# Windowed attention: the products of weights and values for two heads in one matmul, split into two halves of a step

## The chip, the cores and the metric

The kernel runs on one core of a Trainium2 chip. Its engines work side by side, each through its own queue in program order: TensorE (PE in the profile, its weight loads PEld), VectorE (DVE), ScalarE (ACT), GpSimd (POOL) and SyncE (SP), which here only issues DMAs. The metric is the device time of one execution in microseconds (us); lower is better. Matmul results land in PSUM and are copied from there to SBUF by ACT or DVE.

## The reference

The whole is a network of four blocks on 16 sequences of 512 tokens with 128 features. Each block is `x + layernorm(block(layernorm(x)))`. Only the first, an attention with a sliding window, is touched:

```python
H, D, window_size = (16, 64, 32)
B, T, C = x.shape                      # 16, 512, 128
xn = rms_norm(x)
q, k, v = jnp.split(xn @ w_qkv.T, 3, axis=-1)
...
q = apply_rope(q, cos, sin)
k = apply_rope(k, cos, sin)
attn = jnp.einsum('bhqd,bhkd->bhqk', q, k) * scale
mask = (q_pos >= k_pos) & (q_pos - k_pos <= window_size)
attn = softmax(jnp.where(mask, attn, NEG))
out = jnp.einsum('bhqk,bhkd->bhqd', attn, v)
return out.transpose(0, 2, 1, 3).reshape(B, T, H * D) @ w_out.T
```

A query sees itself and the 32 tokens before it. The line that the change is about is the product of `attn` and `v`. After this block come a mixture of eight experts, a second attention and a feed-forward block.

## The kernel before, in words

**Tiling.** `windowed_attention` (from line 296 on) works in units: a unit u is one sequence (u // 2) and one half of its 16 heads, so there are NU = 32. A unit has NP = 4 pairs of heads, p = 0 to 3, and each pair is a step n = 4u + p; there are 128. Queries stand in eight blocks of QT = 64, named by j (0 to 3, of 128 tokens) and c (0 or 1, which half). A block of 64 queries needs KW = 96 keys: its own 64 and the 32 before. All data are float32.

**Values.** `values(u, j)` (L416 on) multiplies tokens by the value weights into pv; ACT copies it to `v_odd` (L423). The 96 keys of a c = 1 block are rows of one `v_odd` tile. Those of a c = 0 block are not, so when j = 3 is done three DMAs on SP's queue (L426, L427, L428) put together `v_even`, a shifted copy. Their calls stand in step p = 0 of the unit that they serve (`values(u, 3)`), the products that read them begin in step p = 3.

**One step n** of the schedule, which is written out by hand at the end of the function, calls in this order:

1. `weigh(n - 1)`: DVE sums the exponentials (L467), takes reciprocals (L469); POOL multiplies (L470).
2. `score(n)`: PE adds the mask and the products of q and k into s (L438, L447); DVE takes the negated row maxima nmax (L452); ACT takes eight exponentials of 128x96 into pr (L458). s has one buffer, so the s of the next step waits for these exponentials.
3. `project(...)`: PE projects a quarter of q or k of a unit further on into pq (L398), DVE multiplies it by cosines and sines (L402, L404), POOL adds (L407), SP writes the result to DRAM (`far`, L408); one step later SP reads it back in another layout into qT or kT (L411). The tile t that far is read from has three buffers.
4. `values(u, 3)` if p = 0, `values(u + 1, 1)` if p = 3, `project_out` (pf, L512) if p is odd.
5. `turn(n - 2)`: PE transposes pr (pt, L481), ACT copies the result to prT (L483). PSUM tiles of pv, pf, pt and some transposes share three buffers.
6. `products(n - 3)`: PE multiplies the weights prT by the values into po (L498), DVE copies po to oT (L502). po has one buffer.
7. `values(u + 1, 0)` if p = 2, `values(u + 1, 2)` if p = 3, and small tasks of layer norms that come due.

So the products of pair n come three steps after its scores. In `products` the two heads r of the pair are separate matmuls: head r has 64 columns of the values as stationary side, its 64 queries as moving side, and writes partitions 64r to 64r + 63 of po. That makes 4 x 2 x 2 = 16 matmuls a step. A float32 matmul shows as two records in the trace, so the profile counts 32 a step.

`project_out(u, part)` later reads oT, all four pairs of a unit, as stationary side. It is not changed.

Of the kernel before, what the change touches and what calls it, by code (L numbers as in the profile page):

```python
# [20 lines left out]
F32 = mybir.dt.float32  # L21
# [10 lines left out]
P = 128  # L32
B, T, C = 16, 512, 128
NTB = T // P
# [5 lines left out]
H0, D0, WIN = 16, 64, 32  # L40
QT = 64
KW = QT + WIN
# [183 lines left out]
def run_due(tasks, now):  # L226

    for task in list(tasks):
        if task[0] <= now:
            lag = next(task[1], None)  # L230
            if lag is None:
                tasks.remove(task)
            else:
                task[0] = now + lag
# [61 lines left out]
def windowed_attention(net):  # L296
# [12 lines left out]
    nc, tc, a = net.nc, net.tc, net.a  # L309
    NU, NP, NC = 2 * B, H0 // 4, H0 * D0 // P  # L310
    HALF = D0 // 2
    with ExitStack() as ctx:
# [9 lines left out]
        with tc.tile_pool(name="wload", bufs=1) as lp, tc.tile_pool(name="ps_w", bufs=2, space=PSUM) as ps:  # L322
# [13 lines left out]
            for g in range(NG):  # L336
# [4 lines left out]
                s = D0 ** -0.5 if g < 2 else 1.0  # L341
# [17 lines left out]
        v_odd = [wp.tile([P, NTB, T], F32, name=f"v_odd{i}") for i in range(2)]  # L359
        v_even = [wp.tile([P, NTB, T], F32, name=f"v_even{i}") for i in range(2)]  # L360
# [14 lines left out]
        ps_o = ctx.enter_context(tc.tile_pool(name="ps0_o", bufs=1, space=PSUM))  # L375
        xnT, ao, oT, pairs, tasks = {}, {}, {}, {}, []
# [4 lines left out]
        def prepare(b):  # L381

            z = tok.tile([P, NTB, C], F32, name=f"z_a{b}", tag="z")
            yield from normed_in(net, net.x[b], f"a{b}", z, by_scalar, 1.0 + RMS_EPS, LN_EPS * RMS_EPS)
            yield 2
            pz = transposed(net, ps_x, z, f"a{b}", "x")
            x = tok.tile([P, T + WIN], F32, name=f"xnT_{b}", tag="xnT")
            nc.scalar.copy(x[:, :T], pz)
            nc.scalar.copy(x[:, T:], pz[:, :WIN])
            xnT[b] = x  # L390
# [39 lines left out]
        def score(n):  # L430

            u, p = divmod(n, NP)
            q, k = qT[u % 2], kT[u % 2]
            s = ps_s.tile([P, 2, T], F32, name=f"s_{n}", tag="s")
            for c in range(2):
                for r in range(2):
                    at = slice(64 * r, 64 * r + 64)
                    nc.tensor.matmul(  # L438
                        s[64 * c : 64 * c + 64, r, : NTB * KW], lhsT=eye[at, at],
                        rhs=mask[at, c].rearrange("p j k -> p (j k)"), start=True, stop=False,  # L440
                    )
            for j in range(NTB):
                for c in range(2):
                    t = j * P + c * 64
                    for r in range(2):
                        at = slice(64 * r, 64 * r + 64)
                        nc.tensor.matmul(  # L447
                            s[64 * c : 64 * c + 64, r, j * KW : (j + 1) * KW], lhsT=q[at, p, t : t + 64],
                            rhs=k[at, p, t : t + KW], start=False, stop=(j == NTB - 1),
                        )  # L450
            nmax = sp.tile([P, 2, NTB], F32, name=f"nmax_{n}", tag="nmax")
            nc.vector.tensor_reduce(  # L452
                nmax, s[:, :, : NTB * KW].rearrange("p r (j k) -> p r j k", k=KW), AX.X, ALU.max, negate=True
            )
            pr = ep.tile([P, 2, NTB, KW], F32, name=f"pr_{n}", tag="pr")
            for r in range(2):
                for j in range(NTB):
                    nc.scalar.activation(  # L458
                        pr[:, r, j, :], s[:, r, j * KW : (j + 1) * KW], AF.Exp, bias=nmax[:, r, j : j + 1]
                    )  # L460
            pairs[n] = pr

        def weigh(n):

            pr = pairs[n].rearrange("p r j k -> p (r j) k")
            sums = sp.tile([P, 2 * NTB], F32, name=f"sums_{n}", tag="sums")
            nc.vector.tensor_reduce(sums, pr, AX.X, ALU.add)  # L467
            rc = sp.tile([P, 2 * NTB], F32, name=f"rc_{n}", tag="rc")
            nc.vector.reciprocal(rc, sums)  # L469
            nc.gpsimd.tensor_tensor(pr, pr, per_token(rc, KW), ALU.mult)  # L470
# [12 lines left out]
                nc.scalar.copy(prT[:KW, c], pt[c][:KW])  # L483
            pairs[n] = prT

        def products(n):
            u, p = divmod(n, NP)
            prT = pairs.pop(n)
            if p == 0:
                oT[u] = up.tile([P, NP, T], F32, name=f"oT_{u}", tag="oT")  # L490
            po = ps_o.tile([P, T], F32, name=f"po_{n}", tag="o")
            for j in range(NTB):
                for c in range(2):
                    v = (v_even, v_odd)[c][u % 2]
                    t = j * P + c * 64
                    for r in range(2):
                        at = (2 * p + r) * D0
                        nc.tensor.matmul(  # L498
                            po[D0 * r : D0 * r + D0, t : t + 64], lhsT=v[:KW, j, at : at + D0],
                            rhs=prT[:KW, c, r, j, :], start=True, stop=True,  # L500
                        )
            nc.vector.tensor_copy(oT[u][:, p, :], po)  # L502

        def project_out(u, part):

# [48 lines left out]
        with tc.manual_schedule():  # L554
            for _ in prepare(0):
                pass
            for n in range(-NP - 2, NP * (NU + 2) + 16):
                u, p = divmod(n, NP)
                if 0 <= n - 1 < NP * NU:
                    weigh(n - 1)  # L560
                if 0 <= n < NP * NU:
                    score(n)
                ahead, k = divmod(n + NP + 2, NP)
                if ahead < NU:
                    kind, g = ((1, 0), (0, 0), (1, 1), (0, 1))[k]
                    task = project(ahead, kind, g)
                    tasks.append([n + next(task), task])
                if 0 <= u < NU and p == 0:
                    values(u, 3)
                if 0 <= u + 1 < NU and p == 3:  # L570
                    values(u + 1, 1)
                if p % 2 and 0 <= u - 2 + p // 2 < NU:

                    project_out(u - 2 + p // 2, 1 - p // 2)
                    if p == 1 and u % 2:
                        tasks.append([n, close((u - 2) // 2)])
                if 0 <= n - 2 < NP * NU:
                    turn(n - 2)
                if 0 <= n - 3 < NP * NU:
                    products(n - 3)  # L580
                if 0 <= u + 1 < NU and p >= 2:
                    values(u + 1, 2 * (p - 2))
                if p == 0 and u % 2 and (u + 3) // 2 < B:
                    tasks.append([n, prepare((u + 3) // 2)])
                run_due(tasks, n)
            assert not tasks
# [904 lines left out]
```

## Time and profile before

| what | us |
|---|---|
| median of 3 runs | 2530.02 |
| lowest and highest of them | 2494.01, 2530.4 |
| the profiled execution's own time | 2521.29 |
| its span, first to last instruction | 2518.7 |

The mean clock granted to TensorE in the profiled execution was 0.901 of full speed. The first attention takes nearly the first 1020 us. Three windows of it, by the view of windows: the window, its length, then busy us and number of instructions for PE, PEld, DVE, ACT and POOL, then the granted clock, the share of the DMA engines and GB/s:

```profile
300.00:500.00 200.00, 183.17 (x2657) 122.02 (x2653) 158.48 (x278) 110.74 (x343) 131.36 (x114) 0.98 0.57 175
500.00:700.00 200.00, 186.55 (x2715) 124.69 (x2713) 156.02 (x280) 108.70 (x335) 130.75 (x111) 0.97 0.57 169
700.00:900.00 200.00, 185.74 (x2643) 122.50 (x2642) 156.41 (x279) 113.08 (x348) 129.06 (x109) 0.97 0.56 173
```

The stage is even: the three windows are alike. Groups by line from 300 to 700 us, 54 steps (engine, operation, tiles, shapes, count; busy us in all, mean ns of one; idle us before them and what ended it):

```profile
L498 PE MATMUL po<-prT,v_even 96*64 96x64 f32 x870 | 58.0, 232 | 2.5 <-DMA v_even<-v_odd 2.5
L498 PE MATMUL po<-prT,v_odd 96*64 96x64 f32 x872 | 55.6, 226 | 0.0
L502 DVE COPY oT<-po 128x512 f32<-128x512 f32 x54 | 37.0, 685 | 24.1 <-PE po L498 24.0
L520 ACT COPY ao<-pf 128x256 f32<-128x256 f32 x13 | 5.0, 388 | 3.5 <-PE pf L512 3.5
```

A mean of one matmul includes its way through the array, where it overlaps its neighbours; the time that a group of matmuls takes is read from the timeline or the chain of waits.

### The profile page before, as it was taken

Reading aid. Unit: us, or ns where it says so; the run is one execution under the profiler, and the core shown is the slowest. Engines: PE = TensorE matmul, PEld = TensorE weight load, DVE = VectorE, ACT = ScalarE, POOL = GpSimd, SP = SyncE. Lnnn points to the kernel's source line nnn. Section 1 sums busy time; section 2 is a strip of 40 time slices with the busy share of each in tenths; the row PEclk is TensorE's granted clock in tenths of the full one; section 3 lists DMA queues with packets and bytes.
Section 4 is the critical chain, followed back from the end, with each engine's and each line's share of the span. In section 5 each row is a group of like instructions: output and inputs, shape, how many; then the busy total and the mean of one; then the engine's idle time right before and its main releaser. Section 6 shows DMA issues by size and latency. Waiting matters only on the chain.

```text
span 2518.7 us, 54547 instructions
## 1 busy us (share of the span) xinstructions
PE 2086.6 (83%) x21337; PEld 1215.0 (48%) x21337; DVE 1886.4 (75%) x3732; ACT 1383.0 (55%) x3189; POOL 1360.0 (54%) x1338
## 2 busy tenths in 40 slices
PE   5898989999999998236799269999999999998876
PEld 2565656666666566126689123333333333332544
DVE  4777777777888775487861578888888888881886
ACT  1555555555555555113334127777777777775885
POOL 3566666666666664634442334555555565311888
PEclk8999999999999999555579659999999999995999
DMA  6555555555555554101112233333343323321001
GB/s 185 176 173 160 172 170 167 179 168 171 169 178 175 169 172 141 38 13 27 40 51 79 69 67 90 115 92 91 96 117 101 95 83 106 110 61 34 12 26 34
DMA packets 163900, 275.31 MB, mean 109 GB/s; under 512 B 20226, under 2 KB 64572, under 8 KB 158524
## 3 DMA queue, kind: packets, MB, share of 16 engines
q1 hardware_dynamic: 157632, 259.32, 34.6%
q0 software_dynamic: 4096, 8.40, 1.3%
q10 hardware_dynamic: 1916, 4.12, 0.6%
q8 instruction: 168, 2.75, 0.5%
q14 instruction: 88, 0.72, 0.1%
HBM read 133.49 MB, written 114.03 MB: 98 GB/s over the span
## 4 chain that ended last, share of the span: by engine, by line
PE 35%; DVE 24%; DMA 22%; ACT 10%; POOL 5%; issue 2%; SPq 1%; POOLq 0%; DVEq 0%; ACTq 0%
DMA far<-t 17%; PE po L1183 9%; PE sT L1169 6%; DVE nm L1138 5%; ACT ex L1175 4%; DMA v_even<-v_odd 3%; PE s L1135 3%; PE ph L760 2%; PE pq L398 2%; PE po L760 2%; DVE hit L834 2%; DVE t L402 2%; DVE t L404 1%; PE pqk L1067 1%; PE po L498 1%
## 5 line engine op out<-in xcount | busy, mean ns | idle before, releaser
L1138 DVE TENSOR_REDUCE nm<-s 128x2 f32<-128x1024 f32 x512 | 609.9, 1214 | 71.9 <-PE s L1135 66.9
L1175 ACT ACTIVATE ex<-sT 128x512 f32<-128x512 f32 x1024 | 531.1, 604 | 183.6 <-PE sT L1169 183.2
L407 POOL TENSOR_TENSOR t<-t,t 128x512 f32<-128x512 f32 x256 | 319.9, 1270 | 272.7 <-DVE t L404 264.0
L458 ACT ACTIVATE pr<-s,nmax 128x96 f32<-128x96 f32 x1024 | 251.4, 357 | 316.2 <-DVE nmax L452 282.1
L1169 PE MATMUL sT<-qs,ks 50*128 50x512 f32 x1024 | 348.6, 481 | 62.9 <-ACT ex L1175 62.9
L1135 PE MATMUL s<-ks,qs 48*128 48x512 f32 x1024 | 294.6, 448 | 41.6 <-DVE nm L1138 28.7
L1169 PEld LDWEIGHTS sT<-qs,ks 50*128 50x128 f32 x1024 | 143.3, 189 | 351.2 <-ACT ex L1175 308.0
L1183 PE MATMUL po<-ex,vs 128*32 128x512 f32 x2048 | 283.9, 628 | 0.0
L398 PE MATMUL pq<-xnT,wqk 128*128 128x512 f32 x512 | 264.2, 640 | 21.0 <-DVE t L404 19.5
L402 DVE TENSOR_TENSOR t<-pq,rope 128x1024 f32<-128x1024 f32 x128 | 156.4, 1222 | 111.3 <-DMA far<-t 76.4
L470 POOL TENSOR_TENSOR pr<-pr,rc 128x768 f32<-128x768 f32 x128 | 188.3, 1471 | 49.2 <-DVE rc L469 42.7
L1135 PEld LDWEIGHTS s<-ks,qs 48*128 48x128 f32 x1024 | 123.8, 192 | 71.7 <-DVE nm L1138 47.1
L404 DVE TENSOR_TENSOR t<-pq,rope 128x1024 f32<-128x1024 f32 x128 | 155.4, 1214 | 0.0
L483 ACT COPY prT<-pt 96x512 f32<-96x512 f32 x256 | 138.8, 604 | 22.6 <-PE pt L481 22.5
L498 PE MATMUL po<-prT,v_even 96*64 96x64 f32 x2048 | 136.6, 232 | 16.2 <-DMA v_even<-v_odd 15.1
L419 PE MATMUL pv<-wv,xnT 128*128 128x512 f32 x256 | 148.4, 664 | 0.0
L512 PEld LDWEIGHTS pf<-wo,oT 128*128 128x128 f32 x1024 | 126.9, 196 | 29.8 <-issue 28.6
L398 PEld LDWEIGHTS pq<-xnT,wqk 128*128 128x128 f32 x512 | 89.4, 194 | 107.3 <-issue 88.6
L502 DVE COPY oT<-po 128x512 f32<-128x512 f32 x128 | 87.7, 685 | 68.5 <-PE po L498 68.2
L423 ACT COPY v_odd<-pv 128x512 f32<-128x512 f32 x128 | 79.2, 619 | 95.3 <-PE pv L419 95.2
L498 PE MATMUL po<-prT,v_odd 96*64 96x64 f32 x2048 | 131.5, 227 | 0.0
L512 PE MATMUL pf<-wo,oT 128*128 128x128 f32 x1024 | 127.8, 279 | 0.0
(276 smaller groups left out, 4078.2 us busy)
## 6 DMA issues: line engine op xcount, KB each, us to landing
far<-t SPq DMA_DIRECT2D x256, 256.0 KB
kT<-far SPq DMA_DIRECT2D x64, 512.0 KB
qT<-far SPq DMA_DIRECT2D x64, 512.0 KB
away<-cut SPq DMA_DIRECT2D x64, 256.0 KB
qs<-away SPq DMA_DIRECT2D x64, 256.0 KB
ks<-away SPq DMA_DIRECT2D x128, 128.0 KB
heap<-ou SPq DMA_DIRECT2D x64, 256.0 KB
v_even<-v_odd SPq DMA_DIRECT2D x32, 384.0 KB
```

Source lines behind the costliest of these rows:

```text
L398: nc.tensor.matmul(ps[:, s], lhsT=wqk[:, kind, 2 * half + g, s, :], rhs=xnT[b][:, :T], start=True, stop=True)
L402: nc.vector.tensor_tensor(t1, ps, rope[:, 0:1, :].to_broadcast([P, 2, T]), ALU.mult)
L407: nc.gpsimd.tensor_tensor(t1[:, s], t1[:, s], t2[:, 1 - s], ALU.add if s else ALU.subtract)
L458: nc.scalar.activation(pr[:, r, j, :], s[:, r, j * KW : (j + 1) * KW], AF.Exp, bias=nmax[:, r, j : j + 1])
L470: nc.gpsimd.tensor_tensor(pr, pr, per_token(rc, KW), ALU.mult)
L498: nc.tensor.matmul(po[D0 * r : D0 * r + D0, t : t + 64], lhsT=v[:KW, j, at : at + D0], rhs=prT[:KW, c, r, j, :], start=True, stop=True,)
L512: nc.tensor.matmul(pf[:, i, :], lhsT=o[:, p, j * P : (j + 1) * P], rhs=wo[:, NP * half + p, :], start=(p == 0), stop=(p == NP - 1),)
L1135: nc.tensor.matmul(ps[:, r, :], lhsT=q[rows, s, i * P : (i + 1) * P], rhs=kk[rows, s, :], start=True, stop=True)
L1138: nc.vector.tensor_reduce(nms[b, z][:, :, s, i], ps, AX.X, ALU.max, negate=True)
L1169: nc.tensor.matmul(t, lhsT=kk[rows, s % HQ, i * P : (i + 1) * P], rhs=q[rows, s % HQ, :], start=True, stop=True)
L1175: nc.scalar.activation(e, st[r], AF.Exp, scale=SCALE1)
L1183: nc.tensor.matmul(outs[-1][PADH * j : PADH * (j + 1), :], lhsT=vs[b % 3][:, i, VW * (NJ * g + j) : VW * (NJ * g + j) + PADH], rhs=weights ...
```

## The change

`products` takes both heads of a pair in one matmul. The stationary side is 96 x 128, the values of both heads side by side, and the moving side 96 x 128, the weights of both heads for one block of 64 queries. The result has four quarters, of which only those of a head's own values with its own weights are used, and copied. The copies are four instead of one, each of 64 partitions by 256 elements: three by ACT, one by DVE.

The products come in two halves. `part` 0 (j = 0 and 1) is called straight after the scores' matmuls and nmax, ahead of the exponentials, which now have a function of their own; `part` 1 (j = 2 and 3) stands where the products stood. Each half fills one po tile of 128 x 512, and po still has one buffer.

```diff
@@ in score @@
             nc.vector.tensor_reduce(
                 nmax, s[:, :, : NTB * KW].rearrange("p r (j k) -> p r j k", k=KW), AX.X, ALU.max, negate=True
             )
+            pairs[n] = s, nmax
+
+        def exponentials(n):
+            s, nmax = pairs[n]
             pr = ep.tile([P, 2, NTB, KW], F32, name=f"pr_{n}", tag="pr")
@@ products @@
-        def products(n):
+        def products(n, part):
             u, p = divmod(n, NP)
-            prT = pairs.pop(n)
-            if p == 0:
+            prT = pairs[n]
+            if p == 0 and part == 0:
                 oT[u] = up.tile([P, NP, T], F32, name=f"oT_{u}", tag="oT")
-            po = ps_o.tile([P, T], F32, name=f"po_{n}", tag="o")
-            for j in range(NTB):
-                for c in range(2):
-                    v = (v_even, v_odd)[c][u % 2]
-                    t = j * P + c * 64
-                    for r in range(2):
-                        at = (2 * p + r) * D0
-                        nc.tensor.matmul(
-                            po[D0 * r : D0 * r + D0, t : t + 64], lhsT=v[:KW, j, at : at + D0],
-                            rhs=prT[:KW, c, r, j, :], start=True, stop=True,
-                        )
-            nc.vector.tensor_copy(oT[u][:, p, :], po)
+            po = ps_o.tile([P, 4, 2, QT], F32, name=f"po_{n}_{part}", tag="o")
+            for i in range(4):
+                j, c = 2 * part + i // 2, i % 2
+                nc.tensor.matmul(
+                    po[:, i], lhsT=(v_even, v_odd)[c][u % 2][:KW, j, 2 * p * D0 : 2 * (p + 1) * D0],
+                    rhs=prT[:KW, c, :, j, :], start=True, stop=True,
+                )
+            for r in range(2):
+                rows = slice(D0 * r, D0 * (r + 1))
+                to = oT[u][rows, p, 4 * QT * part : 4 * QT * (part + 1)].rearrange("p (i q) -> p i q", q=QT)
+                if part and not r:
+                    nc.vector.tensor_copy(to, po[rows, :, r, :])
+                else:
+                    nc.scalar.copy(to, po[rows, :, r, :])
+            if part:
+                pairs.pop(n)
@@ the schedule of a step @@
                 if 0 <= n < NP * NU:
                     score(n)
+                if 0 <= n - 3 < NP * NU:
+                    products(n - 3, 0)
+                if 0 <= n < NP * NU:
+                    exponentials(n)
                 ahead, k = divmod(n + NP + 2, NP)
...
                 if 0 <= n - 2 < NP * NU:
                     turn(n - 2)
                 if 0 <= n - 3 < NP * NU:
-                    products(n - 3)
+                    products(n - 3, 1)
```

## The prediction

> **What bounds the kernel now.** I read the page first, then the windows, the groups by line and the waits of the first attention, last the timeline of single steps. The page puts that stage in the first 15 or 16 of the 40 slices:
>
> ```profile
> PE   5898989999999998236799269999999999998876
> DVE  4777777777888775487861578888888888881886
> PEclk8999999999999999555579659999999999995999
> ```
>
> From 60 to 960 us the windows give TensorE (PE) 822.91 of 900 us busy, DVE 694.74, ACT 486.30, POOL 570.82. PE is the busiest by far, and its idle time has few causes. The waits of PE in that stretch:
>
> ```profile
> PE s L438 <- ACT pr L458: 21.0, 27, 2.1
> PE pt L481 <- ACT v_odd L423: 18.8, 15, 1.8
> PE po L498 <- DMA v_even<-v_odd: 14.0, 14, 2.3
> PE tp_e L241 <- ACT prT L483: 13.4, 12, 2.0
> PE pq L398 <- DVE t L404: 7.7, 13, 2.4
> ```
>
> The reader is to see 76 us of real waits in 900, and that one of them is the very matmul that is changed: it waits for a DMA. From 300 to 700 us there are 54 steps (54 nmax reductions), so a step takes 7.41 us; 7.46 us is the mean of the starts of s over nearly the whole stage, so a unit of four steps takes 29.84. The steps are unlike: where PE never waits, a step of p=2 takes 5.58 us and one of p=3 about 9.1. Adding the shortest of each place of a unit gives 26.7 us; the other 3.1 are waits and a halved clock. PE is the bound, with waits on top.
>
> **What the products cost.** A piece of the chain of waits shows PE working through one step, with start and duration in us:
>
> ```profile
> 481.31 0.66 PE s L447 x32
> 481.97 1.91 PE pq L398 x4
> 483.88 1.78 PE pf L512 x16
> 485.67 0.58 PE pt L481 x16
> 486.25 1.11 PE po L498 x32
> ```
>
> A float32 matmul is two records. The old products are 16 matmuls, 32 records, in 1.11 us: 35 ns a record of 64 columns. The row pf streams 128 columns a record at 111 ns. Half of that would be 56, so the two heads, which write different halves of the partitions, run side by side. The new products are 8 matmuls, 16 records, of 128 columns and 128 outputs: the shape of pf except for 96 rows. By that row they take 16 x 0.111 = 1.78 us, two halves of 0.89. PE gets +0.67 us a step, x 128 = +86 us. Half of each product is thrown away; fewer instructions do not pay for it.
>
> Here a rule speaks against the change too. The Trainium skill, page "TensorEngine Tiling (Array Packing)", section "Theoretical Speedup", gives up to 2x to column tiling where the stationary side is 64 wide. Giving the tiling up would then double 1.11, +142 us in 128 steps. The rows make it 1.6x, because the packed form does not reach its ideal; I take the rows, +86.
>
> **What moves.** Evacuation: the DVE copy of 0.685 us (oT, 128x512) becomes three ACT copies and one DVE copy of 64x256. The nearest rows are ACT ao<-pf, 128x256, 388 ns, and DVE ao, 128x256, 410 ns. ACT +1.16 us a step, DVE -0.27. Half the partitions could make them no cheaper (taken) or down to half; a strided read could bring the DVE one back to 0.685. ACT is 54% busy and waits 123 us for nmax in 54 steps, 2.3 a step; this covers the two copies now ahead of the exponentials. Without that cover the exponentials come 0.78 us later, against about 1.5 us between their end and the next s. I cost it at nothing. The DVE relief is worth something only through later waits.
>
> New waits: po has one buffer, now used twice a step. The second half needs the two ACT copies: first half ends 1.9 us into the step, copies by 2.7, second half starts at 4.4: hidden. The first half of the next step needs ACT's third copy, and in the built program that ACT copy waits for the DVE copy; v_odd copies, the next two po copies and the exponentials queue behind it. Path after pq: t 1.22 + t 1.13 + copy 0.41 + ACT 0.39 + handovers 0.1 = 3.3 us; PE has pv 0.96 + pt 0.58 + half 0.89 + s 1.02 = 3.45 in p=0 and p=2, more in p=1 and p=3. It fits by 0.15 us if DVE is on time. DVE is late by waits for far, 26.3 us in 54 steps; if all of it came through in half of the steps or in all: 31 to 62 us for the stage. Steps longer by 0.67 give those DMAs two more microseconds over their three buffers, so I take 0 and keep 62 for the range; below nothing is excluded, as no wait is removed.
>
> **The wait that decides.** The first half now stands right after s, before pq, pv, pf and pt. In p=3 these are products of a new unit, and need all three v_even copies, also for blocks 0 and 1. Timeline, SP's issues, then PE in the p=3 step:
>
> ```profile
> 542.83 1.51 SPq L408 DMA_DIRECT2D far<-t  x2
> 544.40 2.30 SPq L426 DMA_DIRECT2D v_even<-v_odd  x1
> 546.80 0.58 SPq L427 DMA_DIRECT2D v_even<-v_odd  x1
> 547.42 2.81 SPq L428 DMA_DIRECT2D v_even<-v_odd  x1
> ...
> 550.17 0.36 PE L438 MATMUL s<-mask,eye 64*64 64x384 bf16 x4
> ...
> 559.70 0.48 PE L498 MATMUL po<-prT,v_even 96*64 96x64 f32 x4 [0.88 <-DMA v_even<-v_odd]
> ```
>
> The unit began at 531.65. The copies were issued 12.75 us into it and had landed at its 28th, 9.5 us into p=3. By the landings in the trace this is the rule: in even units they are complete 7.0 to 10.5 us into p=3 and the products start at once after; in odd ones at 5.2 to 8.4, where the products are due about 6.0. The new place is 1.0 us into p=3.
>
> What the longer steps give back: p=0 to 2 take 18.3 us at the shortest, then 20.3, so the new place is 21.3 us after the unit's start. The issue follows far of p=0 on SP; its POOL sums are done at s 1.02 + half 0.89 + pq 1.91 + t 2.35 + POOL 2.5 = 8.7 us, far's issue to 9.5. SP is no longer a step behind there, because PE's stall lets it catch up. L427 is issued 2.4 later and lands, by the mean of the trace, 11.8 us after: 23.7. PE waits 2.4 us in every unit, pq and all behind it with it. From there p=3 still has 8.0 us of the rows above (half, pq, pv, pf, pt, half, pv) and some 0.3 of transposes: 32.0 us a unit.
>
> Clock: after idle gaps of 1.75 and 0.88 us in that p=3 the clock is halved. Window, then busy us with counts of PE, PEld, DVE, ACT, POOL, then PEclk, DMA, GB/s:
>
> ```profile
> 556.00:559.50 3.50, 1.06 (x16) 0.72 (x15) 2.42 (x3) 2.52 (x9) 1.43 (x3) 0.80 0.61 195
> 559.50:563.60 4.10, 3.90 (x34) 2.32 (x34) 0.77 (x2) 0.37 (x1) 2.18 (x2) 0.50 0.26 102
> ```
>
> The Trainium skill, "TensorE: Matmul & The Clock Gate", "What's actually happening", halves it only after an idle window of about 3.4 us: by that a stall of 2.4 us costs nothing, by the row a window at half clock, 1.7 us. I take half of it, 0.8: 32.8 us. With the rule it would be 32.0, 25 us less in all.
>
> **Sum.** 32.8 - 29.84 = 2.96 us in 31 units (the first fills) = +92 us. On the profiled execution's 2521.29 us (span 2518.7) that is 2613; that execution is 0.35% under the median of 2530.02, and the runs reach from 2494. The later stages keep their code.
>
> **The rivals.**
> 1. Longer products alone (0.20). SP catches up further or DMAs land sooner, 2.4 us are gained and v_even is in time. PE's 26.7 + 2.7 = 29.4 us a unit, with 0.6 of waits and 0.5 of clock left: 30.5, +21 us, 2542. For: the waits shrink as DVE gets 0.94 us a step more room. Against: the landings above.
> 2. Not slower (0.10): the lengthened PE work fills its waits altogether. 29.4 against 29.84 is -14 us, 2507. It decides if v_even lands by 21.3 us and all 3.1 us of waits and clock loss in a unit go. This is the most that the change can win unless a record of 128 columns takes well under 111 ns; at 70 ns the products would be no longer than before.
> 3. The handover DVE, ACT, po (0.13): with 62 us more, 2675; with the clock halved in each unit some 27 more, 2702.
>
> My forecast has the rest, 0.57, from 2565 to 2655 by itself (a landing 1.5 us earlier or later is 46 us). The range takes in most of rivals 1 and 3: 2535 to 2690. A measurement here can tell about 2% from no change, some 50 us. Slower by more: forecast nearly whole and rival 3 less a little, 0.70 less 0.03, and a strip of rival 1, 0.08: 0.75. Within: the rest of rival 1, most of rival 2 and that strip of the forecast, 0.21. Faster: 0.04.
>
> **What would show it.** Right: new products at 0.11 us a record, 1.78 us a step; a wait of PE's po for v_even in most units, at the front of p=3, 1 to 4 us long; more clock digits below 9; DVE idle share up. Wrong: a po group under 1.3 us a step would void the 86 us; no waits on v_even would mean rival 1; many short waits of po for ACT's oT copy in p=0 and p=2, rival 3.

## The result, and the profile after

| | before | after |
|---|---|---|
| median, us | 2519.39 (9 runs) | 2541.82 (9 runs) |
| lowest and highest, us | 2494.01, 2538.98 | 2533.82, 2552.96 |
| profiled execution, us | 2521.29 | 2547.55 |
| ratio after / before, 95% interval | | 1.0092 (1.0064 to 1.012) |

The kernel became slower by 0.9%, some 22 us, where 92 were forecast. The range held the time and the direction was right, but the number that came, 2542, is that of rival 1. Up to the first operation of the expert routing after the attention the two profiles stand at 1054.9 and 1076.2 us: the 21 us lie in the stage that was changed. (The unchanged stages behind it take 1447 to 1475 us in the various profiles of this study, so small differences below are read from ratios; where a profile is set beside them, it is read up to the routing or over the same steps.)

The page after, PE and the granted clock in 40 slices:

```profile
PE   5899999999999999435789459999999989998886
PEclk8999999999999999655579759999999999996999
```

The digits of PE in the first stage went from 8 and 9 to all 9. PE's waits from 60 to 980 us (releaser: us in all, times, longest):

```profile
PE po L500 <- ACT oT L510: 15.3, 27, 0.8
PE po L500 <- DMA v_even<-v_odd: 10.5, 3, 8.6
PE s L438 <- ACT pr L462: 3.6, 14, 0.6
```

The waits of before for v_odd, prT and t are gone but for a few tenths, the one for pr is down to 3.6 us from 23.6 in the same window. The forecast's wait for v_even shows three times, nearly all of it once, at the very first p=3. One wait is new: the first half of a pair for ACT's copy of the half before, 15 us in all. The window 300 to 700 us (busy us and counts of PE, PEld, DVE, ACT, POOL, then clock, DMA share, GB/s) of before, then of after:

```profile
300.00:700.00 400.00, 369.72 (x5368) 246.70 (x5362) 314.50 (x558) 219.43 (x678) 262.11 (x224) 0.97 0.57 172
```

```profile
300.00:700.00 400.00, 391.62 (x4392) 277.04 (x4383) 295.98 (x548) 275.19 (x821) 255.24 (x219) 1.00 0.56 167
```

PE is busy 98% of the time instead of 92%, at full clock instead of 0.97. The groups of the changed lines there:

```profile
L500 PE MATMUL po<-prT,v_even 96*128 96x128 f32 x422 | 92.4, 301 | 7.2 <-ACT oT L510 7.2
L510 ACT COPY oT<-po 64x256 f32<-64x256 f32 x158 | 57.9, 366 | 59.0 <-PE po L500 43.0 <-DVE oT L508 14.4
```

The last column of ACT's copy shows a side effect: 14.4 us of waiting for DVE's copy of the other rows of the same po.

Where did the time go? Between the starts of s I took the mean of each place in two units (an even and the following odd one, us):

| step | p=0 | p=1 | p=2 | p=3 | p=0 | p=1 | p=2 | p=3 | unit |
|---|---|---|---|---|---|---|---|---|---|
| before | 5.81 | 6.98 | 5.83 | 11.52 | 6.38 | 6.43 | 7.27 | 9.72 | 29.97 |
| after | 6.28 | 8.01 | 6.29 | 9.01 | 6.55 | 8.01 | 6.72 | 9.82 | 30.34 |

Before, the steps vary from unit to unit; after, they are almost constant. Everything became longer but two places: the p=3 step of even units, where before waited for v_even, is 2.5 us shorter, although PE has more to do in it, and the p=2 step of odd units is 0.55 us shorter. The sum over steps 8 to 119: PE's work, which is its busy time less what half clock cost it, from 746.9 to 831.5, +85 us or 0.76 a step; its idle gaps from 66.7 to 18.2, -48; time at half clock from 51.2 us to none, of which half is lost, -26. That is 839.2 to 849.7, +10. The rest of the 21 lies in the filling and draining of the pipeline: 7.2 us more up to step 8, of which 6.0 are the first p=3 step (n = 3), 12.0 us before and 18.0 after, with the 8.6 us of waiting for the first v_even in it; and some 3.6 us more from step 120 to the routing.

### The profile page after: what moved, and what is told of

It reads as the page before. It is cut to its first block, busy times and chain, and to the rows that moved or that the text cites. A ratio compares the mean times of both kernels' runs of the same rounds, so it can differ in the third digit from the quotient of the medians.

```text
span 2545.8 us, 50760 instructions
## 1 busy us (share of the span) xinstructions
PE 2159.5 (85%) x19289; PEld 1304.1 (51%) x19289; DVE 1855.0 (73%) x3732; ACT 1530.6 (60%) x3573; POOL 1357.5 (53%) x1338
## 4 chain that ended last, share of the span: by engine, by line
PE 54%; DVE 22%; ACT 12%; POOL 4%; DMA 4%; issue 3%; SPq 1%; another core or an unknown queue 0%; POOLq 0%; ACTq 0%; DVEq 0%
PE po L1197 9%; PE po L500 8%; PE pq L398 7%; PE sT L1183 6%; DVE nm L1152 5%; PE pf L522 4%; ACT ex L1189 4%; PE s L1149 3%; PE pv L419 3%; PE pt L485 2%; PE ph L774 2%; PE po L774 2%; ACT pr L462 2%; DVE hit L848 2%; PE s L447 2%
## 5 line engine op out<-in xcount | busy, mean ns | idle before, releaser
L398 PE MATMUL pq<-xnT,wqk 128*128 128x512 f32 x512 | 250.5, 613 | 12.5 <-DVE t L404 11.8
L500 PE MATMUL po<-prT,v_even 96*128 96x128 f32 x1024 | 225.0, 302 | 30.6 <-ACT oT L510 20.1
L510 ACT COPY oT<-po 64x256 f32<-64x256 f32 x384 | 140.8, 367 | 163.6 <-PE po L500 121.3
L500 PE MATMUL po<-prT,v_odd 96*128 96x128 f32 x1024 | 199.0, 276 | 0.0
L500 PEld LDWEIGHTS po<-prT,v_even 96*128 96x128 f32 x1024 | 154.8, 191 | 59.5 <-ACT oT L510 28.6
L500 PEld LDWEIGHTS po<-prT,v_odd 96*128 96x128 f32 x1024 | 156.4, 193 | 0.0
L419 PE MATMUL pv<-wv,xnT 128*128 128x512 f32 x256 | 131.2, 594 | 0.0
```

The lines of the kernel that those rows point to most:

```text
L398: nc.tensor.matmul(ps[:, s], lhsT=wqk[:, kind, 2 * half + g, s, :], rhs=xnT[b][:, :T], start=True, stop=True)
L419: nc.tensor.matmul(pv, lhsT=xnT[b][:, WIN + j * P : WIN + (j + 1) * P], rhs=wv[:, half * T : (half + 1) * T], start=True, stop=True,)
L500: nc.tensor.matmul(po[:, i], lhsT=(v_even, v_odd)[c][u % 2][:KW, j, 2 * p * D0 : 2 * (p + 1) * D0], rhs=prT[:KW, c, :, j, :], start=True, ...
```

## The experiments

All runs are of variants of the two kernels; ratios are to the kernel before. Letters for theories are those of each expectation; the text says in words what they stand for. Where no window is named, PE's waits are those from 60 to 980 us and SP's those from 300 to 700 us. For the readings below one needs to know how SP shows that it is late. SP issues read-backs (L411) and `far` (L408) in turn; a read-back, whose call comes at the end of a step, fetches not the `far` sent just before it but the one before that. If SP is up to date it waits at L408 for POOL's sum. If it is a step behind, the sum is there long before, L408 goes at once behind the read-back, and SP then stands at the next L411 for the landing of the earlier `far`. SP's waits, 300 to 700 us, of before and then of after:

```profile
SPq L411 <- DMA far<-t: 139.9, 50, 5.5
SPq L408 <- POOL t L407: 22.9, 15, 3.3
```

```profile
SPq L408 <- POOL t L407: 135.3, 77, 5.2
SPq L411 <- DMA far<-t: 72.0, 31, 3.7
```

Before is behind in most steps, after is up to date in most. v_even's copies are queued on SP behind these two.

### 1. The early half without the wider products

`after` with each head's products separate again (64 columns), still in halves with four copies.

```diff
+                for r in range(2):
+                    nc.tensor.matmul(
+                        po[D0 * r : D0 * (r + 1), i, r, :], lhsT=v[:KW, j, at : at + D0],
+                        rhs=prT[:KW, c, r, j, :], start=True, stop=True)
```

> The changed kernel in everything but the matmul: per head again, 64 columns each, written into the same quarters of po, in the same two halves and places, with the same four copies. Theory A (TensorE's streaming is the bound; the merged matmul costs 0.67 us a step and most of it is seen): the unit of four steps falls from 30.4 us by up to 2.7, at best -86 us against the changed kernel; but its p=3 then begins some 2 us earlier against v_even, which in the changed kernel lands 2 us before it is needed, so waits of po for v_even come back in part. About 2470 us, 50 to 90 below the changed kernel. Theory B (the early place of the first half is what costs, through v_even or the copies): v_even waits of 2 us or more in every unit, time at or above the changed kernel, 2540 or more. Theory C (the number of instructions counts): 16 more matmuls a step make it slower than the changed kernel.

Measured: 2527.99 us, ratio 1.0013 (0.9978 to 1.0049). PE's waits, 60 to 980 us:

```profile
PE po L503 <- ACT oT L513: 22.1, 32, 0.8
PE s L438 <- ACT pr L462: 20.9, 31, 1.4
PE po L503 <- DMA v_even<-v_odd: 15.1, 5, 7.6
```

SP was up to date here too (136.0 us at L408 for POOL), v_even landed 9.4 us after the issue of L427, and still nothing was won: waits for the copies and for the exponentials took the place of those that went. The expected 2470 missed. So the early half on its own, with these four copies, is worth nothing. What the wider products cost on top of it is 14 us by the medians (2541.82 - 2527.99), 20 by the ratios, as the two rounds had different medians of before, and 11 by the profiles up to the routing: between half and nearly all of the 22 us, and far less than the 74 us that they add to PE's work between these two kernels (0.58 us a step).

### 2. The added PE time alone

`before` with three extra 128-column matmuls a step, 6 records, whose result is written over. 6 x 111 ns = 0.67 us were meant; in the trace they add 0.87 us a step (the shortest p=2 step goes from 5.58 to 6.44), 111 us in all.

```diff
+            for _ in range(3):
+                nc.tensor.matmul(
+                    po[:, :P], lhsT=v_odd[u % 2][:KW, 0, 2 * p * D0 : 2 * (p + 1) * D0],
+                    rhs=prT[:KW, 1, :, 0, :], start=True, stop=True)
```

> The kernel before with three extra 96x128 by 128-column matmuls a step ahead of the products, into po, overwritten by them: 6 records of 0.11 us, the 0.67 us that the merged products add, and nothing else changed. Theory A (most of the added TensorE time is absorbed because longer steps fill waits on ACT, DVE, v_even and the halved clock): +15 to +40 us over the kernel before, clock near 1.0 in the first attention. Theory B (the waits were removed by the new evacuation and order, not by the length): waits stay, +70 to +90 us.

Measured: 2532.1 us, ratio 1.0027 (0.9987 to 1.0067): some +7 us, where 15 to 40 were expected, for 111 us of work on the busiest engine. The window 300 to 700 us and SP's largest wait in it:

```profile
300.00:700.00 400.00, 397.33 (x5569) 275.29 (x5568) 302.10 (x547) 217.23 (x668) 257.09 (x221) 1.00 0.56 169
```

```profile
SPq L411 <- DMA far<-t: 141.5, 52, 5.6
```

PE went from 369.72 to 397.33 us busy and from 0.97 to full clock; its gaps over steps 8 to 119 fell from 66.7 to 7.2 us, and these steps took 851.2 us for 839.2: 12 of the 97 us added in them are seen. The added work fell into the waits. But SP stayed behind exactly as in before, with v_even's copies landing 11.2 us after issue: steps that are longer through PE alone do not bring SP up to date. They only make PE late enough for v_even.

### 3 and 4. The four copies

The copies by ACT and DVE in `before` (3), and in `after` the order of the second half's two copies swapped, so that ACT's comes first (4).

```diff
@@ 3, from before @@
-            nc.vector.tensor_copy(oT[u][:, p, :], po)
+            for half in range(2):
+                for r in range(2):
...
+                    if half and not r:
+                        nc.vector.tensor_copy(oT[u][rows, p, cols], po[rows, cols])
+                    else:
+                        nc.scalar.copy(oT[u][rows, p, cols], po[rows, cols])
@@ 4, from after @@
-            for r in range(2):
+            for r in (1, 0):
```

> The kernel before with its one DVE copy of po replaced by three copies by ACT and one by DVE of 64x256 each, at the old place, matmuls unchanged. Theory A (TensorE is the bound and DVE's relief of 0.27 us a step reaches it only through waits): within -30 and +10 us of the kernel before, as ACT's 1.16 us a step lie ahead of the v_odd copies that pt waits for. Theory B (DVE's load is what makes the waits): -40 us or more.

Measured: 2555.88 us, ratio 1.0123 (1.0063 to 1.0183). PE's waits:

```profile
PE s L438 <- ACT pr L458: 38.8, 42, 1.9
PE pt L481 <- ACT v_odd L423: 20.5, 24, 1.5
PE tp_e L241 <- ACT prT L483: 20.1, 13, 1.7
```

Every wait for ACT grew. Three copies more on ACT, on the old schedule, cost 31 us, where -30 to +10 were expected. That is at least as much as the whole change (the intervals of the two ratios overlap); experiment 1 has the same four copies in its early halves and costs 3 (0.13%), so the early place pays for most of them. SP caught up from about unit 9 on, with no product ahead of pq, and with steps that had become long through waits for ACT; that alone was no gain.

> The changed kernel with the two copies of a half issued in the other order, head 1 first: ACT's third copy then waits for TensorE instead of for the DVE copy. Theory A (what is left of TensorE's idle time in the changed kernel is po waiting for that handover, 15.3 us between 60 and 980 us): -8 to -16 us against the changed kernel. Rival (another wait takes its place at once, as the exponentials still come after nmax): no change, within 4 us.

Measured: 2582.05 us, ratio 1.0214 (1.0149 to 1.028): slower, not faster. The wait that I wanted to remove changed sides, as DVE's copy then waits for ACT's, and the next half for DVE:

```profile
PE po L500 <- DVE oT L508: 25.5, 26, 1.2
```

DVE's own idle time shows its side of it (300 to 700 us):

```profile
L508 DVE COPY oT<-po 64x256 f32<-64x256 f32 x51 | 21.3, 417 | 73.5 <-ACT oT L510 73.5
```

Whichever copy is issued second waits for the first. Here DVE stands 1.4 us a step before its copy, where in `after` ACT stood 14.4 us in the whole window. That this is what makes it 40 us slower than `after`, through the work that queues on DVE behind the copy, is argued only. The handover of rival 3 exists, at 15 us in `after` and 26 here, where 62 were the bound.

### 5 and 6. DVE's relief, and two copies instead of four

Experiment 5 gives the one copy of `before` to ACT. Experiment 6 is experiment 1 with 128 x 256 tiles, so that each half is one copy, the first by ACT, the second by DVE.

```diff
@@ 5, from before @@
-            nc.vector.tensor_copy(oT[u][:, p, :], po)
+            nc.scalar.copy(oT[u][:, p, :], po)
@@ 6, from experiment 1 @@
+            po = ps_o.tile([P, T // 2], F32, name=f"po_{n}_{part}", tag="o")
...
+            if part:
+                nc.vector.tensor_copy(to, po)
+            else:
+                nc.scalar.copy(to, po)
```

> The kernel before with its DVE copy of po (0.685 us) made by ACT instead, one copy of the same 128x512, about 0.6 us; nothing else changed. Theory A (SP's queue ran a step behind because DVE was late with t: DVE relief alone lets SP catch up): v_even lands about 9 us after its issue instead of 14, SP waits for POOL more than for far; time 10 to 30 us under the kernel before. Theory B (what unbunches SP is that ACT delays the loop, as in the run with four copies at the old place): SP catches up too, but waits on ACT make it slower than before by 10 us or more. Theory C: SP stays behind, within 5 us of before.

Measured: 2517.45 us, ratio 0.9982 (0.9945 to 1.0019). SP's waits and PE's largest:

```profile
SPq L411 <- DMA far<-t: 137.0, 50, 5.4
```

```profile
PE po L498 <- DMA v_even<-v_odd: 36.1, 27, 3.8
```

DVE with 0.69 us a step less to do does not bring SP up to date, so the smaller load of DVE in `after` is not what did it. The wait for v_even grew instead.

> Per-head matmuls in two halves at the places of the changed kernel, but each half in its own 128x256 po tile with one copy, the first by ACT, the second by DVE; ACT has 0.39 us more a step than before instead of 1.16, and no copy waits for another engine's copy. Theory A (in the run with small matmuls in halves the gain of 0.67 us of TensorE time was lost to ACT's three short copies and their handover from DVE): the po and s waits for ACT, 43 us there, fall under 15, and the time is 2470 to 2500. Rival (v_even is the next bound, as p=3 now begins before it has landed): po waits for v_even of 1 us or more in most units, 2510 or more.

Measured: 2511.95 us, ratio 0.9961 (0.9926 to 0.9996). Half the copies made of experiment 1 a kernel slightly faster than before; 2470 to 2500 were expected. SP is up to date (106.8 us at L408); PE still waits 26.1 us for pr and 20.4 for v_even. Against `after` it is 30 us less: the wider products and the copies that their quarters need cost that much together.

### 7 and 8. v_even off SP, and v_even late

```diff
@@ 7, from before, likewise the other two @@
-                nc.sync.dma_start(out=even[:64, 1:, :], in_=odd[64:, : NTB - 1, :])
+                nc.scalar.dma_start(out=even[:64, 1:, :], in_=odd[64:, : NTB - 1, :])
@@ 8, from after: the three copies, now shift(u), one step later @@
                     values(u, 3)
+                if 0 <= u < NU and p == 1:
+                    shift(u)
```

> The kernel before with the three v_even copies issued from ACT's queue, right behind the v_odd copy that they need, instead of from SP's behind far. Theory A (SP being a step behind is what makes v_even late and TensorE wait in p=3): the po waits for v_even vanish, 20 to 50 us under the kernel before. Rival (the v_odd and exponentials' waits of p=3 take over, or ACT's time for issuing delays the exponentials): within 10 us of before.

Measured: 2507.33 us, ratio 0.9954 (0.9921 to 0.9986). That is some 12 us under before, where 20 to 50 were expected. The wait for v_even vanished, and ACT, which issues the copies now, is waited for:

```profile
PE s L438 <- ACT pr L458: 31.4, 29, 9.0
PE pt L481 <- ACT prT L483: 28.5, 29, 5.4
```

SP was up to date without the three copies in its queue (185.7 us at L408 for POOL).

> The changed kernel with the three v_even copies issued one step later on SP, behind far of p=1, so some 6 us later. Theory A (the prediction's mechanism is right and only its landing time was wrong: v_even lands some 2 us before the first half in p=3 needs it): po then waits about 4 us for v_even in each unit, +100 to +170 us over the changed kernel, and the clock is halved after many of these waits. Rival (the wait is absorbed elsewhere): +40 us or less.

Measured: 2773.6 us, ratio 1.1017 (1.0949 to 1.1085), 232 us over `after`, where 100 to 170 were expected. PE's wait, 60 to 980 us:

```profile
PE po L501 <- DMA v_even<-v_odd: 134.0, 24, 14.9
```

The waits are 5.6 us in the mean, where 4 had been expected. From 300 to 700 us the p=3 steps took 15.6 to 17.5 us, and the granted clock there was 0.91. So the forecast's mechanism is real: in `after` the early half does stall the whole step if v_even is not there. It was the arrival that I had wrong.

### 9 and 13. What brings SP up to date

In `before`, one product is called right after score(n), ahead of pq: once, at n = 3 (9), or in every p=3 step (13).

```diff
@@ 9 @@
                     score(n)
+                if n == 3:
+                    products(0)
@@ 13 @@
                     score(n)
+                if 0 <= n - 3 < NP * NU and p == 3:
+                    products(n - 3)
```

> The kernel before with a single call moved: the very first products, of pair 0, are called right after the scores of step 3 instead of at that step's end; all other steps are as before. Theory A (SP's queue has two lasting states, and a first half placed ahead of pq makes TensorE wait once for the first v_even, some 8 us, in which SP catches up for good): from step 4 on SP waits for POOL between a read-back of far and the next far, v_even lands 9 us after issue, the v_even waits are gone; 10 to 30 us under the kernel before. Rival (the early place must be kept in each unit to hold that state): SP is behind again within a few units, time within 8 us of before.

Measured: 2511.98 us, ratio 0.9958 (0.9922 to 0.9995). SP's largest wait, 300 to 700 us:

```profile
SPq L411 <- DMA far<-t: 137.4, 52, 5.3
```

SP was up to date in unit 1 and behind again from unit 2 or 3: a single catching up does not last.

> The kernel before with the whole of its products called right after the scores in the p=3 step of every unit, and at the old place in the three other steps; matmuls and the DVE copy as before. Theory A (a product that waits for v_even ahead of pq holds back the next far, so that SP catches up in each unit and stays so): SP waits for POOL between the read-back and far, v_even lands about 9 us after its issue, the v_even waits are short; 5 to 30 us under the kernel before. Rival (something else in the changed kernel, as the length of its steps or its copies, holds the state): SP is behind again after some units, v_even lands 11 us or more after issue, and the waits for it at the front of p=3 make it 30 us or more slower than before.

Measured: 2509.12 us, ratio 0.9995 (0.996 to 1.0031). SP's waits, then PE's:

```profile
SPq L408 <- POOL t L407: 111.1, 81, 5.6
SPq L411 <- DMA far<-t: 99.4, 43, 3.9
```

```profile
PE s L438 <- ACT pr L458: 37.8, 34, 2.2
PE po L498 <- DMA v_even<-v_odd: 24.6, 11, 8.7
```

With the early product in each p=3, SP holds, and v_even lands 9.4 us after issue. A reason offers itself: if v_even is late, PE stalls before pq, so that no new `far` comes and SP catches up; where the product stands behind pq, pv and the rest, the stall comes too late for that. This reason is argued only; that in `before` the place in each p=3 holds SP up to date, and one single time does not, is shown by the pair. It is not the only way: in experiments 3, 7 and 12 SP is up to date with no product ahead of pq. And it was worth no time here: PE waits for ACT instead.

### 10 and 11. v_even asked for earlier

The call `values(u, 3)` moves ahead of `project`, so SP has the three copies in its queue before `far` of p = 0: from `before` (10), and from experiment 6 (11).

```diff
@@ 10 @@
                     score(n)
+                if 0 <= u < NU and p == 0:
+                    values(u, 3)
                 ahead, k = divmod(n + NP + 2, NP)
...
-                if 0 <= u < NU and p == 0:
-                    values(u, 3)
```

> The kernel before with the call that ends in the v_even copies moved ahead of the projection within step p=0, so SP issues them before far of that step instead of behind it. Theory A (v_even is late because it queues on SP behind far and the read-back ahead of it): it is issued some 2 us earlier or more and the po waits for it fall to a third; 5 to 25 us under the kernel before. Rival (SP, still behind, waits there for ACT's v_odd copy and delays far, so t waits more for far): no gain, or slower by up to 15 us.

Measured: 2473.03 us, ratio 0.9814 (0.9748 to 0.988): the fastest of all, faster than both kernels, and by more than the 5 to 25 us expected. In the profiles 31 of the 47 us lie ahead of the routing (1024.2 us for 1054.9); the other 17 lie in the unchanged stages behind it and are not explained. SP's first two issues of the copies in a unit that begins at 546.06 and whose p=3 begins at 568.46, then PE's largest wait:

```profile
555.23 0.53 SPq L426 DMA_DIRECT2D v_even<-v_odd  x1
555.86 0.57 SPq L427 DMA_DIRECT2D v_even<-v_odd  x1
```

```profile
PE s L438 <- ACT pr L458: 38.0, 36, 2.8
```

The copies go ahead of far (issued at 558.49), at 9.2 us into the unit, and land 9.1 after L427's issue: no wait for v_even is left. A step takes 7.24 us in the mean. SP itself is still a step behind, with no wait for t's sum at L408:

```profile
SPq L411 <- DMA far<-t: 179.2, 81, 4.7
```

So v_even need not wait for SP to catch up; it is enough that its copies no longer stand behind `far`.

> Per-head matmuls in two halves with one copy each (the run e6), with the v_even copies ahead of the projection as in e10. Theory A: the v_even waits that e6 kept at the start and in some p=3 go, 5 to 15 us under e6, about 2500. Rival (s and the transposes waiting for ACT set the pace there): within 5 us of e6.

Measured: 2484.31 us, ratio 0.9861 (0.9798 to 0.9925), with 25.8 us of waiting for pr and 4.9 for v_even: 28 us under experiment 6, where 5 to 15 were expected. The halves add nothing to the move.

### 14 and 15. The same move with the added PE time

> The changed kernel with the v_even copies ahead of the projection in step p=0, the edit that took 47 us off the kernel before. Theory A (the changed kernel is held by TensorE and no longer waits for v_even): within 15 us of the changed kernel, 2525 to 2550. Rival (v_even or SP still cost it something): 25 us or more faster than the changed kernel.

`after` with the edit of experiment 10: 2537.65 us, ratio 1.0071 (1.0029 to 1.0112), 4 us under `after`, with overlapping intervals. Past the first p=3, v_even costs `after` next to nothing, as its trace said; the first p=3 step fell from 18.0 to 13.7 us.

> The kernel before with the v_even copies ahead of the projection (e10) and the three extra matmuls a step of e2. Theory A (with the wait for v_even gone, added TensorE time is seen far more than the 7 us that e2 cost the kernel before): +40 to +80 us over e10. Rival (other waits absorb it as well): under +25 us.

Experiment 10 with the extra matmuls of experiment 2: 2523.82 us, ratio 1.0038 (1.0002 to 1.0074). PE was busy 398.14 of 400 us from 300 to 700 us.

This is 51 us over experiment 10, where the same matmuls added some 7 us to `before`. In the profiles, over steps 8 to 119, it is 845.4 us for 811.4: 34 of the 97 us added there, where experiment 2 showed 12. Without the stall for v_even about three times as much of the added work is seen, but not all: PE's gaps fell from 50.0 to 4.0 us. The two kernels with them, experiments 2 and 15, both come to PE 99% busy and to nearly the same time: the work fills the waits, whatever their cause, up to the point where PE is full.

### 12. The early half put late

`after` with the first half moved to just before `turn(n - 2)`.

```diff
@@ from after @@
                     score(n)
-                if 0 <= n - 3 < NP * NU:
-                    products(n - 3, 0)
...
+                if 0 <= n - 3 < NP * NU:
+                    products(n - 3, 0)
                 if 0 <= n - 2 < NP * NU:
                     turn(n - 2)
```

> The changed kernel with its first half moved back from behind the scores to just before the transposes; matmuls and copies as in the changed kernel. Theory A (the early place is what lets SP catch up): SP stays behind at least for the first units, v_even lands 13 us and more after issue, po waits for v_even at p=3 in the first units, and po's second half waits up to 0.5 us for the ACT copies; 0 to 25 us over the changed kernel. Rival (the four copies alone do it): SP catches up as quickly as in the changed kernel, time within 8 us of it.

Measured: 2680.2 us, ratio 1.0623 (1.0545 to 1.07), where 0 to 25 us over `after` were expected. PE's wait:

```profile
PE po L500 <- ACT oT L510: 82.7, 102, 2.5
```

With the two halves near each other the second finds the one po buffer occupied: the first half's copies stand behind the exponentials on ACT. The early place of the first half, which I had treated as a risk, is what gives the copies their time. The expectation missed on SP too. It had SP stay behind; SP was further ahead than in `after`, and v_even's copies landed 9.0 us after the issue of L427:

```profile
SPq L408 <- POOL t L407: 220.8, 81, 7.6
```

So in `after` the early place is not needed to bring SP up to date: the four copies do it as well, with the longer steps that came with them (8.8 us here, 7.7 in experiment 3).

## Why the prediction was right and wrong

**PE's added work: right.** Forecast +0.67 us a step by the row of pf, measured +0.71 (the shortest p=2 step, 5.58 to 6.29) and +0.76 in the mean of all steps. The timeline after, around a p=3 step (start, us):

```profile
563.61 0.36 PE L438 MATMUL s<-mask,eye 64*64 64x384 bf16 x4
564.55 0.49 PE L500 MATMUL po<-prT,v_even 96*128 96x128 f32 x2
565.55 1.88 PE L398 MATMUL pq<-xnT,wqk 128*128 128x512 f32 x4
567.27 1.02 PE L419 MATMUL pv<-wv,xnT 128*128 128x512 f32 x2
```

A half takes 1.00 us from start to start, a little more than 0.89; the pq behind it takes 1.72 instead of 1.91. The doubling that the Trainium skill's "TensorEngine Tiling (Array Packing)", "Theoretical Speedup", allows for was not seen: +0.71 where it made +1.11. The group by itself, two halves of 1.00 for 1.11, grew 1.8 times; the faster pq behind it takes part of that back.

**"The wait that decides": the step that failed.** The prediction had v_even land 23.7 us into the unit, needed at 21.3: 2.4 us of wait and 0.8 of clock in every unit. SP after, in the unit whose s begins at 542.97:

```profile
550.56 1.74 SPq L408 DMA_DIRECT2D far<-t  x2
552.36 0.53 SPq L426 DMA_DIRECT2D v_even<-v_odd  x1
552.99 1.20 SPq L427 DMA_DIRECT2D v_even<-v_odd  x1
554.23 2.72 SPq L428 DMA_DIRECT2D v_even<-v_odd  x1
```

L426 was issued 9.4 us in; forecast 9.5. The need came at 564.55, 21.6 us in; forecast 21.3. But L427 followed L426 by 0.6 us, not 2.4, and landed 9.1 us after its issue, not 11.8 (median of units 2 to 29, by the semaphores in the trace; 11.6 in before). That is 10.0 + 9.1 = 19.1 us. L428 lands 0.2 us later; over units 1 to 31 the last of the three copies was there 2.2 us (median) ahead of the need, with hardly a wait and no lost clock. The error is a mixed state: I let SP be up to date for the time of the issue, and took the durations of issue and landing from a trace in which SP was behind and its transfers ran one straight after another. What stood just ahead in the queue matters more than whether SP is late: in experiment 10, with SP still behind but the copies issued behind the read-back alone, L426 took 0.5 us and L427 landed 9.1 us after its issue; in experiment 14, where SP waits some 4 us for v_odd ahead of L427, it landed after 5.4. Of the size of the step, experiment 8 is the check: with L427 issued 6.7 us later (median), the forecast wait comes in nearly every unit.

**SP catches up: right in fact, wrong in reason.** The prediction gave PE's stall in every unit as the reason, and rival 1 spoke of longer steps. After the first p=3 `after` hardly waits for v_even, and SP stays up to date. Experiment 2 shows that more PE time does not do it, 5 that DVE's relief does not; 13 shows that an early product in each p=3 is enough in `before`, 3 and 12 that the four copies, with longer steps, do it without one. Which of the two does it in `after` is not separated.

**The sum.** 32.8 us a unit were forecast, 30.34 measured. Without the 2.4 and 0.8 it is 29.6, and 0.7 is left; PE's remaining gaps, 18.2 us in 28 units, are 0.65 of it. Rival 1 had 30.5 us and 2542, and its unit is the one that came; but that its total fits to the microsecond is luck. It kept 0.5 us of lost clock that was not there, and had 29.4 us of PE's work where 29.7 were measured. Over steps 8 to 119 the kernel lost 10 us, half of its +21; the other half came from the fill and the drain, which the prediction put at nothing ("the first fills"), and of which the first wait for v_even is the largest part. A slip in the working did no harm: 18.3 us for p=0 to 2 "at the shortest" is no minimum (the shortest steps add to 17.9 us in even units and 17.7 in odd ones).

**Evacuation.** ACT's copies took 366 ns for the 388 taken, DVE's 412 for 410. The handover, costed at nothing with 62 us as the bound, came to 15 us in 27 places. Its cover is the early place of the first half: without it the copies cost what experiments 3 and 12 show.

**Clock.** 0.8 us of loss a unit was forecast; there was none, for the stalls it came from were absent. What a stall of 2.4 us does by itself, other traces show. The granted clock changes only at the ends of intervals of 3.41 us. In experiment 10 PE stood 2.27 us within one such interval, in a single wait, and the next ran at half clock (window, length, busy us and counts of PE, PEld, DVE, ACT and POOL, clock, DMA share, GB/s):

```profile
785.43 0.36 PE L438 MATMUL s<-mask,eye 64*64 64x384 bf16 x4 [2.27 <-ACT pr L458]
```

```profile
783.00:786.41 3.41, 1.14 (x43) 0.99 (x39) 3.38 (x6) 3.00 (x11) 1.88 (x2) 1.00 0.34 130
786.41:789.82 3.41, 3.41 (x7) 1.47 (x5) 2.40 (x6) 2.83 (x9) 3.21 (x3) 0.50 0.71 217
```

Over all 17 traces, from the first s to the last, the intervals at full clock divide by PE's idle time in them. With 2.0 us or more, all 107 were followed by one at half clock; with 1.5 to 2.0, 90 of 119; with less, 6 of 3816. So the prediction's row was the better guide than the rule of an idle window of 3.4 us: a stall of 2.4 us that falls within one interval halves the clock in the next, which costs up to 1.7 us (half of 3.41, an estimate for a PE that is busy all through it), and one that is shared between two may cost nothing. In the unit that the prediction shows, the 1.75 us gap alone did it: the half clock begins at 558.09, ahead of the gap of 0.88.

**Open.** What holds SP in its state; and the division of the 22 us between wider products (11 to 20, by experiment 1) and four copies in halves, whose own ratio includes 1. On SP one more figure is on hand: the second `far` of a step landed 12.8 us after its issue in `before` (median) and 9.6 in `after`. Late landings hold back the read-backs, and a late SP sends its transfers close together; that the two keep each other going is a guess that no run here tests.

## What to carry to other kernels

A wait in a loop with a queue behind is a state of the loop, not a constant of the operation: before adding its duration to a schedule, ask what stood just ahead of it in the queue when that duration was measured. An engine that is 92% busy and waits for something late can take on a tenth more work (0.87 us in a step of 7.5, experiment 2) for almost nothing, as its waits and its time at half clock go; but that work fills the room that a cure of the wait would have won: here the better edit moved one call ahead of another in a step, and won 1.2 to 2.5%, of which 1.2% show in the stage itself. A change that makes a wait vanish in the steady loop can still pay it once in the fill. Where a single buffer is used twice in a step, look first at which queue its copies stand in, and how far apart the two uses are.

## What the runs showed of the hardware

- The same DMA took longer to issue and land with more just ahead of it in the queue: 2.3 us to issue L426 and 11.6 us to land L427 where a read-back and `far` had gone straight before (`before`), 0.5 and 9.1 where only one of the two had (`after`, experiment 10), and 5.4 to land L427 where some 4 us had passed without an issue (experiment 14).
- 8 matmuls of 128 columns over the whole array cost 2.0 us, 1.8 net of the quicker pq behind them, against 1.11 for 16 narrow ones: less than twice.
- The granted clock changed only at the ends of intervals of 3.41 us. An interval with 2.0 us or more without work on PE was followed by one at half clock in 107 of 107 cases, one with less than 1.5 us in 6 of 3816.
- Copies by ACT and DVE of different rows of one PSUM tile into one SBUF tile do not run side by side in this program: the second waits for the first, in either order (14.4 us of ACT's waits in 400 us; 73.5 us of DVE's after the order is swapped).
